# A graph layer with gathered edges: the sums and the turns of a bank of sums ahead of the second layer instead of behind it

## The chip, the core and the metric

The kernel runs on one core of one Trainium2 chip. The metric is the device time of one execution in microseconds (us). Names of the engines: PE is TensorE's matmul side and PEld its weight loads, DVE is VectorE, ACT is ScalarE, POOL is GpSimd, SP is SyncE.

## What is computed

A graph with 6250 nodes of 128 numbers and 100000 edges, sorted by destination (more edges fall on low nodes). Each edge runs a three-layer network on its two nodes; the results are averaged by destination; each node runs a two-layer network on itself and its average; a residual and a layer norm follow.

```python
msg_in = jnp.concatenate([node_features[row], node_features[col]], axis=-1)
h = jax.nn.relu(msg_in @ Wm1 + bm1)              # first layer, 256 -> 256
h = jax.nn.relu(h @ Wm2 + bm2)                   # second layer, 256 -> 256
messages = h @ Wm3 + bm3
agg = jax.ops.segment_sum(messages, col, num_segments=num_nodes)
count = jax.ops.segment_sum(jnp.ones(...), col, num_segments=num_nodes)
agg = agg / jnp.clip(count, 1.0)[:, None]
node_in = jnp.concatenate([node_features, agg], axis=-1)
upd = jax.nn.relu(node_in @ Wn1 + bn1) @ Wn2 + bn2
x = _layernorm(x + node_features + upd)
```

## The kernel before, in words

The product of the first layer is split by node: the product with the source half is made once for every node (a table of 256 numbers a node, `atab`), and so is the one with the destination half (`btab`). An edge needs only the row of its source, and the row of its destination. Since the third layer is linear, the second layer's results are summed by destination before it, and it is applied once a node.

The edges go in 196 groups of 512, one group a step. In step k of the main loop stand, in the order in which the program writes them:

- the **first layer** of group k (`first_layer`): 16 transposes of gathered source rows (L569) into two banks of PSUM, then the **destination products** (L582): rows of `btab` ("terms"), spread to the edges by a matrix of zeros and ones ("oht"). ScalarE applies the relu and makes h1 (L588).
- the gather of the source rows of group k+2 (four indirect DMAs on POOL, L533; four buffers of rows), and, at even steps, the next matrices of zeros and ones on VectorE (L547, L552, `make_hot`).
- the **second layer** of group k-1 (`second_layer`, L596): eight matmuls into two banks, each evicted by VectorE (L598) to a buffer of h2. There are six such buffers, used in turn.
- a stage of the **node work** where one is due (`node_step`: L700, L715, L719, L727 are its matmuls).
- **turns** (`turn_sums`): a finished bank of sums, copied out by ScalarE before (L609), is transposed on TensorE by three matmuls (L617, `turned`). VectorE then adds its windows of 32 nodes into the accumulator `acc` (L624, `add_up`, up to four adds), at places that it loads into registers first (L627).
- **rounds of sums** (`some_sums`, L604): the h2 of up to four windows, each multiplied by its own matrix of zeros and ones that is 32 nodes wide, so that four windows share one bank. There is one such bank in the pool for sums (`p3`). After the last round ScalarE copies the bank out.
- every fourth step, up to step 91, two blocks of the table of destination rows: L904 on TensorE, and their split into three parts on ACT and VectorE (L256 to L260).

How many edge tiles share a window sets the stage. In **quads** (groups 0 to 71, and 184 to 191 at the end) a window takes the four tiles of a group: a bank serves four groups and is summed in four rounds. In **pairs** (72 to 147) a window takes two tiles: a bank serves two groups, two rounds. In **singles** (148 to 183) a bank serves one group in one round. `deal` writes down the step of each round; the turn comes one step after the last round, and a table of due steps for the node stages follows from that.

The order on TensorE, ACT and VectorE is the order of the program. On SP (loads of terms and places, stores) and POOL a scheduler sets it.

Of the kernel before, what the change touches and what calls it, by code (L numbers as in the profile page):

```python
# [36 lines left out]
def kernel(  # L37
# [44 lines left out]
    NG = -(-E // GE)  # L82
# [16 lines left out]
    GL = NG - 2 * LATE  # L99
# [199 lines left out]
    with tc.tile_pool(name="prep", bufs=1) as prep, tc.tile_pool(name="pp", bufs=3, space=PSUM) as pp, tc.tile_pool(  # L299
# [11 lines left out]
        with tc.high_priority():  # L311
# [8 lines left out]
            for n in (4, 8, 8, 8, 8, 8):  # L320
                n = min(n, NTF - t)
# [193 lines left out]
    with edge, tc.tile_pool(name="wk", bufs=2) as wk, tc.tile_pool(  # L515
# [29 lines left out]
        def hot_rows(rb):  # L545
            oht = wk.tile([P, 2, HE], BF16, name="oht")
            nc.vector.tensor_scalar(oht, rb, iota_p, None, op0=ALU.is_equal)  # L547
            return oht
# [91 lines left out]
        def make_hot(p):  # L640
            ohts[p] = hot_rows(rels[p // 2][:, 2 * (p % 2):2 * (p % 2) + 2])
            make_nodes(p)
# [115 lines left out]
        def deal(gs, n, steps):  # L758

            steps = list(steps)  # L760
            for t, k in enumerate(steps):
                rounds.setdefault(k, []).append((gs, t, n))
            at = steps[-1] + 1
            turns_at.setdefault(at, []).append(gs[0])
            added.update({g: at + 1 for g in gs})

        for r0, r1, n in REGIONS:
            m = min(n, GT)
            for g in range(2 * r0, 2 * r1, m):
                if n == GT:  # L770
                    deal(range(g, g + n), n, (g + 4, g + 5, g + 6, g + 6))
                elif n == 1:
                    deal([g], n, (g + 3,))
                elif r1 == PAIRS:
                    deal(range(g, g + n), n, (g + 3, g + 4))
                elif g + n < NG:
                    deal(range(g, g + n), n, (NG - 1, NG - 1))
# [24 lines left out]
        def turn_sums(k):  # L802
            for g in turns_at.pop(k, ()):
                part, nw = parts.pop(g)
                pt = turned(part, nw)
                add_up(pt, load_bases(uniti[0:1, unit_at[g]:unit_at[g] + nw], nw, ENG.DVE))
# [50 lines left out]
        for g in range(-4, NG + 14, 2):  # L857
            for i in range(g + 4, min(g + 6, NG)):
                terms[i] = fetch(load_bases(tilei[0:1, i * GT:(i + 1) * GT], NTS[i], ENG.SP), nk_of(i))
            if g < -2:  # L860
                continue
            if (g + 2) % 4 == 0 and g + 6 < NG:
                rels[(g + 6) // 4] = places((g + 6) // 4)
            if g < 0:
                continue
            if g == 0:
                first_step()
            for k in (g, g + 1):
                if k < NG:
                    s = st[k] = {}  # L870
                    if k == 1:
                        xts[1] = open_layer(None, NTS[1], xts[1])
                    s["h1"] = first_layer(rows.pop(k, None), terms.pop(k), ohts[k // 2][:, k % 2], NTS[k], nk_of(k),
                                          xts.pop(k, None))
                    if k == 0:
                        next_rows()
                    if k == 2:
                        nc.scalar.copy(*pace(5))
                if 2 * XS <= k + 2 < NG:
                    rows[k + 2] = gather(sources(k + 2))  # L880
                if k % 2 == 0 and k + 2 < NG:
                    make_hot(k // 2 + 1)
                if 0 <= k - 1 < NG:
                    second_layer(st.pop(k - 1)["h1"], h2s[(k - 1) % len(h2s)], NTS[k - 1])
                if k < NG:
                    node_step(k)
                if k <= NG:
                    turn_sums(k)
                some_sums(k)
                if k > NG:  # L890
                    turn_sums(k)
                if k % 2 == 0 and 2 <= k and k + 5 < NG:
                    nc.vector.tensor_copy(*pace(k + 5))
                if k >= NG:
                    node_step(k)
            if g < 6:
                clear(8)
            if g == 0:
                more_rows()
            t0 = B_EARLY + (g - B_FROM) // 2  # L900
            if g >= B_FROM and (g - B_FROM) % 4 == 0 and t0 < NT:
                pbt = bank()
                for a in range(min(2, NT - t0)):
                    nc.tensor.matmul(pbt[:, a, :], xT[:, (t0 + a) * P:(t0 + a + 1) * P], w1[:, 1, :],  # L904
                                     start=True, stop=True)
                b_terms(t0, pbt, b_rows, b_rest)
            if g == 18:
                late_weights()
            if g == 60:
                made_weights()  # L910
            if g == NG + 2:
                with tc.high_priority():
                    again = nc.values_load(
                        again_i[0:1, 0:1], min_val=0, max_val=1,
                        skip_runtime_bounds_check_because="0 or 1, by its computation")
# [77 lines left out]
```

## Time and profile before

| | us |
|---|---|
| median of 3 runs | 1343.81 |
| the runs | 1333.75 to 1348.66 |
| the profiled execution's own time | 1338.36 |
| its span, first to last instruction | 1336.6 |
| granted clock of TensorE, mean | 0.981 |

How to read the lines shown below: a group's line has source line, engine, operation, output tile <- input tiles, partitions x elements, how often; behind the bar the busy time in us, the mean duration of one in ns, and the idle time of its engine just before it with what ended it. "issue" is time in which the engine waited for nothing that the profile shows, "remote" a releaser that it doesn't know. In the timeline a line starts with its start and its length in us, and merges like instructions (x16). A matmul in f32 has two records, so the eight of a second layer read x16 and a round of four sums x8. The ends of matmuls are modelled, so lengths overlap; starts are what is compared.

### The profile page before, as it was taken

The numbers are of one execution on the slowest core, as the hardware profiler recorded it, in microseconds if no ns is written. First come the engines' busy times: TensorE is split into PE (matmuls) and PEld (weight loads), VectorE is DVE, ScalarE is ACT, GpSimd is POOL, SyncE is SP. The second block draws the span as 40 slices with busy tenths as digits, with TensorE's granted clock in tenths as the row PEclk, the third lists the DMA queues.
The fourth block names the chain that finished last, engine by engine and source line by source line (L and its number), as shares of the span: only waits on it lengthen the run. The fifth ranks groups of instructions, "written<-read, shape, count | busy, mean of one in ns | idle before, by whom it ended". The sixth has DMA issues, their size and how long they took to land.

```text
span 1336.6 us, 27771 instructions
## 1 busy us (share of the span) xinstructions
PE 1236.1 (92%) x10031; PEld 925.5 (69%) x10032; DVE 618.2 (46%) x1551; ACT 441.9 (33%) x1102; POOL 748.7 (56%) x795
## 2 busy tenths in 40 slices
PE   9779998998999999999899999999999999999997
PEld 7556666666666666676677777777777777777675
DVE  6443333433334333434466554444445556556553
ACT  4432323323323323333333423333233333333331
POOL 2366665665665666656555465565655555555550
PEclk9879999999999999999999999999999999999998
DMA  8544434444434434434444344444444434443330
GB/s 287 177 125 134 132 108 127 130 115 129 133 106 128 135 107 125 134 106 131 126 118 119 114 125 128 118 120 129 118 118 118 115 109 118 109 123 110 106 91 4
DMA packets 107617, 163.90 MB, mean 123 GB/s; under 512 B 26367, under 2 KB 71549, under 8 KB 107457
## 3 DMA queue, kind: packets, MB, share of 16 engines
q0 software_dynamic: 37504, 102.29, 27.7%
q1 hardware_dynamic: 69425, 59.50, 14.0%
q8 instruction: 82, 1.34, 0.4%
q14 instruction: 62, 0.51, 0.1%
q10 hardware_dynamic: 544, 0.26, 0.1%
HBM read 142.48 MB, written 19.86 MB: 121 GB/s over the span
## 4 chain that ended last, share of the span: by engine, by line
PE 89%; issue 7%; DVE 2%; another core or an unknown queue 1%; DMA 1%; ACT 0%; SPq 0%; DVEq 0%
PE bank L596 54%; PE bank L569 9%; PE sum_bank L604 9%; PE bank L582 4%; PE bank L617 2%; PE pbt L431 2%; PE bank L727 2%; PE bank L700 2%; PE bank L719 2%; PE bank L715 2%; PE bank L904 1%; PE pt L448 0%; DVE acc L660 0%; DVE x_sb L598 0%
## 5 line engine op out<-in xcount | busy, mean ns | idle before, releaser
L596 PE MATMUL bank<-w,h 128*128 128x256 f32 x3128 | 768.7, 392 | 67.2 <-issue 64.6
L596 PEld LDWEIGHTS bank<-w,h 128*128 128x128 f32 x3128 | 581.7, 192 | 212.3 <-issue 131.1
L533 POOL DMA_INDIRECT rows<-atab,srcT x392 | 374.9, 956 | 260.6 <-issue 90.4
L533 POOL DMA_INDIRECT rows<-atab,srcP x384 | 364.2, 949 | 277.9 <-issue 126.5
L588 ACT ACTIVATE h<-bank,b 128x256 f32<-128x256 f32 x782 | 306.5, 476 | 395.6 <-remote 189.3
L598 DVE TENSOR_TENSOR x_sb<-bank,nb 128x512 f32<-128x512 f32 x263 | 181.0, 691 | 401.7 <-PE bank L596 233.7
L598 DVE TENSOR_TENSOR h_more<-bank,nb 128x512 f32<-128x512 f32 x128 | 88.3, 692 | 177.5 <-PE bank L596 75.0
L569 PEld LDWEIGHTS bank<-ident,rows 64*128 64x128 f32 x3096 | 112.7, 140 | 77.7 <-issue 56.8
L569 PE MATMUL bank<-ident,rows 64*128 64x64 f32 x3096 | 139.3, 230 | 0.0
L624 DVE TENSOR_TENSOR acc<-acc,bank 128x96 f32 x382 | 96.7, 253 | 51.7 <-PE bank L569 16.5
L604 PE MATMUL sum_bank<-x_sb,oh 128*32 128x257 f32 x1044 | 104.1, 393 | 3.0 <-issue 1.6
L609 ACT COPY part<-sum_bank 128x257 f32<-128x257 f32 x96 | 35.8, 373 | 197.0 <-PE bank L582 75.4
L582 PE MATMUL bank<-oht,terms 64*128 64x128 bf16 (+1 forms) x1132 | 82.6, 237 | 14.5 <-issue 10.9
L604 PE MATMUL sum_bank<-h_more,oh 128*32 128x257 f32 x512 | 59.1, 391 | 1.2 <-DVE h_more L598 0.6
L604 PEld LDWEIGHTS sum_bank<-x_sb,oh 128*32 128x32 f32 x1044 | 28.1, 108 | 41.7 <-issue 34.1
L582 PEld LDWEIGHTS <-terms 64*128 64x128 bf16 x1132 | 44.1, 97 | 16.1 <-issue 13.8
L617 PE MATMUL bank<-ident,part 128*128 128x128 f32 (+1 forms) x291 | 47.3, 271 | 0.5 <-ACT part L609 0.5
L745 ACT ACTIVATE y<-y,sh,rs 128x128 f32<-128x128 f32 (+3 forms) x50 | 22.1, 487 | 67.0 <-DVE sh L743 26.6
L695 DVE RECIPROCAL x_sb<-x_sb 128x256 f32<-128x256 f32 (+3 forms) x26 | 43.0, 1655 | 0.9
L617 PEld LDWEIGHTS bank<-ident,part 128*128 128x128 f32 (+1 forms) x291 | 36.6, 139 | 9.3 <-ACT part L609 1.0
L552 DVE TENSOR_TENSOR oh<-iota_n,dloc 128x256 f32<-128x256 f32 x98 | 40.8, 417 | 3.6 <-ACT dloc L838 3.6
L737 ACT ACTIVATE sd<-mv,eps 128x2 f32<-128x2 f32 (+3 forms) x26 | 7.7, 295 | 97.6 <-DVE mv L735 49.5
(157 smaller groups left out, 625.0 us busy)
## 6 DMA issues: line engine op xcount, KB each, us to landing
terms<-btab SPq DMA_DIRECT2D x566, 32.0 KB
places<-reltab SPq DMA_DIRECT2D x98, 128.0 KB
btab<-x_sb SPq DMA_DIRECT2D x10, 768.0 KB
rows<-atab,srcT POOLq DMA_INDIRECT x392
atab<-acc SPq DMA_DIRECT2D x12, 512.0 KB
rows<-atab,srcP POOLq DMA_INDIRECT x384
xr<-in_x_dram SPq DMA_DIRECT2D x23, 128.0 KB
out_dram<-y SPq DMA_DIRECT2D x23, 128.0 KB
```

The costliest lines, as they stand in the source:

```text
L533: nc.gpsimd.indirect_dma_start(out=ag[:, j, :], out_offset=None, in_=atab[:, :], in_offset=bass.IndirectOffsetOnAxis(ap=idx[:, j:j + 1], a ...
L552: nc.vector.tensor_tensor(oh[:, :ng].rearrange("p g j n -> p (g j) n"), iota.to_broadcast([P, ng * GT, WN]), dl.rearrange("p (j o) -> p j ...
L569: nc.tensor.matmul(ph[h][:, c, u * NQ:(u + 1) * NQ], ag[halves[h], u, c * P:(c + 1) * P], ident[halves[h], halves[h]], is_transpose=True, ...
L582: nc.tensor.matmul(ph[h][:, c, k * n:(k + 1) * n], bw[halves[h], k, c * P:(c + 1) * P], oht[halves[h], k * n:(k + 1) * n], start=False, st ...
L588: nc.scalar.activation(h1[:, c, h * HE:(h + 1) * HE], ph[h][:, c, :], AF.Relu, bias=b1[:, c:c + 1])
L596: nc.tensor.matmul(ph2[:, j - j0, :], h1[:, c, j * P:(j + 1) * P], w2[:, c, :], start=(c == 0), stop=(c == HC - 1))
L598: nc.vector.tensor_tensor(h2[:, j0:j0 + 2, :H], ph2, nb2.to_broadcast([P, 2, H]), op=ALU.max)
L604: nc.tensor.matmul(pg[w * WN:(w + 1) * WN, :H + 1], oh, h2, start=(t == 0), stop=(t == total - 1), skip_group_check=True)
L609: nc.scalar.copy(part[:nw * WN], pg[:nw * WN, :H + 1])
L617: nc.tensor.matmul(pt[:, c, :q], rows, ident[:q, :q], is_transpose=True, start=True, stop=True, skip_group_check=True)
L624: nc.vector.tensor_add(window, window, pt[:, :, j * WN:(j + 1) * WN])
L695: nc.vector.reciprocal(rc, rc)
```

## The change

Two places change. In the loop the turns and rounds of a step now stand between the first layer of group k and the second layer of group k-1; they stood behind that second layer and the node stage. In the last steps (k above 196) the turns keep their place behind the rounds. And in quads, whose rounds came at steps g+4, g+5, g+6 and g+6 (g is the first of four groups), they now come one step later, at g+5, g+6, g+7 and g+7; in the quads at the end (group 184 and up) they come at g+5, g+5, g+6 and g+6. Rounds in pairs and singles keep their step.

```diff
@@ -768,7 +768,7 @@
                 if n == GT:
-                    deal(range(g, g + n), n, (g + 4, g + 5, g + 6, g + 6))
+                    deal(range(g, g + n), n, (g + 5, g + 6, g + 7, g + 7) if g < GL else (g + 5, g + 5, g + 6, g + 6))
                 elif n == 1:
@@ -880,13 +880,13 @@
                 if k % 2 == 0 and k + 2 < NG:
                     make_hot(k // 2 + 1)
+                if k <= NG:
+                    turn_sums(k)
+                some_sums(k)
                 if 0 <= k - 1 < NG:
                     second_layer(st.pop(k - 1)["h1"], h2s[(k - 1) % len(h2s)], NTS[k - 1])
                 if k < NG:
                     node_step(k)
-                if k <= NG:
-                    turn_sums(k)
-                some_sums(k)
                 if k > NG:
                     turn_sums(k)
```

The first place is TensorE in the singles, a step with the first stage of a node piece; h is the second layer's input, w its weights, part a bank of sums that was copied out. Before:

```order
L582 MATMUL bank<-oht,terms 128x128
L596 MATMUL bank<-w_151,h_13457 128x256 x8
L700 MATMUL bank<-acc,w_152 128x256 x2
L617 MATMUL bank<-ident,part 128x128 x3
L604 MATMUL sum_bank<-h_more,oh 32x257 x4
L569 MATMUL bank<-ident,rows 128x64 x16
```

And now:

```order
L582 MATMUL bank<-oht,terms 128x128
L617 MATMUL bank<-ident,part 128x128 x3
L604 MATMUL sum_bank<-h_more,oh 32x257 x4
L596 MATMUL bank<-w_151,h_13457 128x256 x8
L700 MATMUL bank<-acc,w_152 128x256 x2
L569 MATMUL bank<-ident,rows 128x64 x16
```

Turn and sums moved from behind the second layer and the node matmuls to between the destination products and the second layer.

The second place is VectorE in the quads, around the split of two blocks of the destination table (L257, L260) and the turn of a bank (L624); bank holds the second layer's product in L598. Before:

```order
L624 ISA
L624 TENSOR_TENSOR acc<-acc,bank 128x3x32
L257 TENSOR_TENSOR x_sb<-bank,x_sb 128x512
L260 TENSOR_TENSOR x_sb<-x_sb 128x2x256
L547 TENSOR_SCALAR oht<-places,iota_p 128x512
L552 TENSOR_TENSOR oh<-iota_n,dloc 128x256
L598 TENSOR_TENSOR x_sb<-bank,nb_155 128x2x256 x2
L893 COPY srcP<-srcT 128x4
```

And now:

```order
L257 TENSOR_TENSOR x_sb<-bank,x_sb 128x512
L260 TENSOR_TENSOR x_sb<-x_sb 128x2x256
L547 TENSOR_SCALAR oht<-places,iota_p 128x512
L552 TENSOR_TENSOR oh<-iota_n,dloc 128x256
L627 TENSOR_LOAD starts_i
L624 ISA
L624 TENSOR_TENSOR acc<-acc,bank 128x3x32
```

Behind these follow three more such adds, and then the two evictions L598: the adds went from the end of one step to ahead of the evictions of the next.

## Prediction

> **What bounds the kernel now.** I read the page first: busy time by engine, the chain of work that ended last, and the costliest groups.
>
> ```profile
> span 1336.6 us, 27771 instructions
> PE 1236.1 (92%) x10031; PEld 925.5 (69%) x10032; DVE 618.2 (46%) x1551; ACT 441.9 (33%) x1102; POOL 748.7 (56%) x795
> PE 89%; issue 7%; DVE 2%; another core or an unknown queue 1%; DMA 1%; ACT 0%; SPq 0%; DVEq 0%
> L596 PE MATMUL bank<-w,h 128*128 128x256 f32 x3128 | 768.7, 392 | 67.2 <-issue 64.6
> L604 PE MATMUL sum_bank<-x_sb,oh 128*32 128x257 f32 x1044 | 104.1, 393 | 3.0 <-issue 1.6
> L598 DVE TENSOR_TENSOR x_sb<-bank,nb 128x512 f32<-128x512 f32 x263 | 181.0, 691 | 401.7 <-PE bank L596 233.7
> L609 ACT COPY part<-sum_bank 128x257 f32<-128x257 f32 x96 | 35.8, 373 | 197.0 <-PE bank L582 75.4
> ```
>
> TensorE (PE) is the chain: 89% of it, and nearly all the rest is "issue", which falls on the second layer, L596. No other engine is near full. The change takes no instruction off TensorE, so what counts is what the new order does to its gaps.
>
> The next view is busy time by stretch, for the transposes of L569 alone. A step has 16 of them, so the count gives the steps of a stretch. The stretches are quads, pairs without node work, pairs with it, and singles.
>
> ```profile
> 95.50:529.90 434.40, 49.91 (x1120) 40.35 (x1120) 0.99 0.42 124
> 529.90:649.80 119.90, 13.57 (x304) 10.97 (x304) 0.97 0.43 124
> 649.80:1028.10 378.30, 40.61 (x912) 32.81 (x912) 1.00 0.42 120
> 1028.10:1243.60 215.50, 22.79 (x504) 18.41 (x504) 1.00 0.41 114
> ```
>
> A step takes 434.4/70 = 6.21 us in the quads, then 6.31, 6.64 and 6.84. The granted clock is 0.97 to 1.00, so the clock explains none of it.
>
> How much of a step is matmul work shows in the timeline of the quads. Here are TensorE's weight loads, and the start of each group of four gathers on GpSimd.
>
> ```profile
> 380.11 0.46 PEld L617 LDWEIGHTS bank<-ident,part 128*128 128x128 f32 x3
> 386.12 0.16 PEld L604 LDWEIGHTS sum_bank<-x_sb,oh 128*32 128x32 f32 x8 [0.33 <-issue]
> 386.69 0.57 PEld L569 LDWEIGHTS bank<-ident,rows 64*128 64x128 f32 x16 [0.41 <-issue]
> 387.55 3.32 PEld L596 LDWEIGHTS bank<-w,h 128*128 128x128 f32 x16 [0.21 <-issue]
> ...
> 390.28 0.94 POOL L533 DMA_INDIRECT rows<-atab,srcP  x1 [1.29 <-PE bank L596]
> 391.77 0.58 PEld L569 LDWEIGHTS bank<-ident,rows 64*128 64x128 f32 x16 [0.41 <-issue]
> 396.35 0.94 POOL L533 DMA_INDIRECT rows<-atab,srcT  x1 [1.38 <-remote]
> ```
>
> From 386.69 to 391.77 a step takes 5.08 us. Two groups of gathers start 6.07 us apart meanwhile (390.28 and 396.35). So a short quad step is quicker than something that keeps a beat of about 6.1 us, and TensorE runs ahead and gives it back as "issue" gaps. What sets the beat the trace does not say. That matters below: work saved or added on TensorE in a stage with such gaps need not show in full.
>
> **The change part by part.** First, shapes. A group of matmuls runs in one of three array shapes: 64\*128 (L569, L582: first layer), 128\*128 (L596, turns L617, node work, L904) and 128\*32 (sums, L604). In the rows above each load that opens a new shape waits 0.21 to 0.41 us, and L617, which follows L596 in the same shape, shows no wait. The price is read from starts on TensorE, in three places:
>
> ```profile
> 501.57 0.49 PE L617 MATMUL bank<-ident,part 128*128 128x128 f32 x3
> 501.89 1.03 PE L904 MATMUL bank<-w,xT 128*128 128x256 f32 x4
> 502.86 0.72 PE L569 MATMUL bank<-ident,rows 64*128 64x64 f32 x16
> ...
> 528.85 1.13 PE L904 MATMUL bank<-w,xT 128*128 128x256 f32 x4
> 529.92 0.71 PE L569 MATMUL bank<-ident,rows 64*128 64x64 f32 x16
> ...
> 891.27 0.71 PE L569 MATMUL bank<-ident,rows 64*128 64x64 f32 x16
> 892.13 3.72 PE L596 MATMUL bank<-w,h 128*128 128x256 f32 x16
> 895.69 0.49 PE L617 MATMUL bank<-ident,part 128*128 128x128 f32 x3
> 896.11 0.64 PE L604 MATMUL sum_bank<-x_sb,oh 128*32 128x257 f32 x8
> 896.68 0.71 PE L569 MATMUL bank<-ident,rows 64*128 64x64 f32 x16
> ```
>
> Three L617 take 0.32 us to the next group of their shape (501.57 to 501.89) and 0.42 to a group of another (895.69 to 896.11): leaving costs 0.10. Four L904 take 0.97 us behind L617 (501.89 to 502.86) and 1.07 where sums stand ahead of them (528.85 to 529.92): entering costs 0.10. A change of shape costs 0.20.
>
> A step with sums and no turn has three changes in both orders: 128\*128, 128\*32, 64\*128 before; 128\*32, 128\*128, 64\*128 now. Nothing is gained or lost, if the one neighbourhood that the trace does not show (L582 straight into L604) is like the others; at 0.1 us more or less for each of the 95 such steps it is -9.5 to +9.5 us, and I take 0, since each of the changes that are shown costs about the same. A step with turn and sums had its turn next to the second layer, in one shape; now turn (128\*128), sums (128\*32) and second layer (128\*128) alternate, four changes for three. Such a step, 5.41 us long (891.27 to 896.68), becomes 5.61. Counted over the program's order, the changes go from 574 to 641. The 67 more lie in the pairs and singles, where turns and sums share a step; in the quads the turn has a step of its own. 67 x 0.20 = +13.4 us on TensorE, with bounds of 0 (all of it inside gaps) and 67 x 0.25 = 16.8.
>
> The Trainium skill, TensorEngine Tiling (Array Packing), section Tiling Modes, says that changing the tiling mode, not merely the tile, drains TensorE. The trace agrees, at the 0.20 us above.
>
> How much of that is hidden? These are TensorE's waits in the stretch of pairs with node work (first two) and in the singles (last two):
>
> ```profile
> PE bank L596 <- issue: 11.4, 20, 1.2
> PE bank L582 <- issue: 5.4, 9, 1.2
> ...
> PE bank L596 <- issue: 6.5, 12, 0.9
> PE bank L582 <- issue: 3.7, 5, 1.2
> ```
>
> That is 16.8 us over 57 steps and 10.2 over 31.5, 0.3 a step, more than the 0.20 or, with pairs, the 0.10 a step that is added. But many steps there carry node matmuls and show no gap, and nothing hides work in those. I take half: 6.7 us paid.
>
> Second, the sums' own wait. The first round of a quad needs the eviction (L598) of the second layer that TensorE has just finished. In a bad step:
>
> ```profile
> 503.72 3.72 PE L596 MATMUL bank<-w,h 128*128 128x256 f32 x16
> 507.37 0.41 PE L604 MATMUL sum_bank<-x_sb,oh 128*32 128x257 f32 x2
> 507.45 0.69 DVE L598 TENSOR_TENSOR h_more<-bank,nb 128x512 f32<-128x512 f32 x1 [0.56 <-PE bank L596]
> 508.19 0.62 PE L604 MATMUL sum_bank<-h_more,oh 128*32 128x257 f32 x2 [0.19 <-issue]
> 508.74 0.58 PEld L569 LDWEIGHTS bank<-ident,rows 64*128 64x128 f32 x16 [0.41 <-PE bank L596]
> ```
>
> The eviction ends at 508.14, and the last sums follow at 508.19. From 507.37 to 508.74 is 1.37 us for a group that takes 0.57 (896.11 to 896.68): 0.80 lost. The waits of this stage are these:
>
> ```profile
> PE sum_bank L604 <- issue: 2.2, 9, 0.5
> PE sum_bank L604 <- DVE h_more L598: 0.6, 2, 0.4
> ```
>
> Eleven times 0.80 is 8.8 us; with one in each of the 18 quads it would be 14.4. Now the first round comes a step later, behind the first layer (386.69 to 387.55: 0.86 us), which covers 0.80. But the turn moves too: its four adds into acc (L624) now stand in VectorE's queue ahead of those two evictions, in the very step whose eviction the round needs.
>
> ```profile
> 381.13 1.12 DVE L624 TENSOR_TENSOR acc<-acc,bank 128x96 f32 x4
> ```
>
> Where the adds have not begun by the time the second layer's first bank is full, 1.12 us comes on top, and the cover is gone. Also this is the stage with the 6.1 us beat. I take half the gain, -4.4, bounds 0 and -14.4. VectorE's register load for the adds (L627) moves with them; it has no busy row, and in the row above the adds follow the eviction at once, so I give it nothing.
>
> Third, small things. At the end, the sums of the last group had a turn and other sums (1 us) between them and the last second layer; now nothing, so they wait for an eviction of 0.69 us and its start: +0.9. Where quads give way to pairs, the last round of a quad and the first of a pair fall in one step and share the one sum buffer, so a copy of 0.37 (L609) stands between: +0.4. The copy, one step ahead of its turn as before, has a whole second layer (3.56 us, 892.13 to 895.69) as cover. On SyncE half of some loads of places and the stores of out come one load of terms or one group later; they are fetched steps ahead, and I give that 0. No node stage begins in another step: their due steps lie behind the sums' end either way.
>
> Sum: 6.7 - 4.4 + 0.9 + 0.4 = +3.6 us on 1338.4 us, the profiled execution's own time (span 1336.6 and 1.8 around it). That execution lies 5.4 us under the median of the runs, 1343.8. So I forecast 1343.8 + 3.6 = 1347 us.
>
> **The rivals.**
>
> *Every shape change is paid (slower).* Place: the 67 steps of pairs and singles with turn and sums. If the gaps of those stages stay beside the new work instead of taking it in, all 13.4 to 16.8 us is added, and if the eviction behind the adds keeps the sums waiting, nothing comes back. With 1.3 for the small things: 1343.8 + 16 = 1360 us. It decides from the point where the shape changes paid, less the waits won, exceed 12.1 us (1% of the run is 13.4, and 1.3 come from the small things). For it: steps with node work have no gap. Against it: 0.3 us of gap a step. Chance 0.28. The rule of the Trainium skill on tiling modes (TensorEngine Tiling (Array Packing), Tiling Modes) would give this outcome, if nothing hid the drains.
>
> *The sums fill the gap (faster).* The sums need nothing fresh and stand where TensorE goes over to the second layer; in the quads L596 carries most of the "issue" time. If the sums' wait goes whole (-9 to -14) and the later second layer meets fewer gaps, with half of the shape changes hidden, the sum is -8 to -20; at -16 it is 1328 us. Against it: gathers at 6.1 us, whose beat an order on TensorE does not obviously touch. Chance 0.24.
>
> *The beat rules (no change).* The quads keep 6.21 us whatever TensorE does there, and half the shape changes show: +8, 1352 us. The forecast and this one together: 0.48.
>
> **How the numbers follow.** Within 1% of 1343.8, about what a measurement of this kernel can tell from no change, means 1330 to 1357. The forecast and the beat lie there: 0.48. Faster by more than 1% is the second rival, 0.24, and slower the first, 0.28. The likeliest case by itself spans 1338 to 1355. For 8 in 10 the range has to reach into both rivals: 1327 to 1361 us, which holds the paid shape changes up to 16.8 and the filled gap down to -16.
>
> **What would show it.** Right: in the singles a turn-and-sum step of about 5.6 us where it was 5.41, with L617 to L604 still at 0.42 and 0.10 more ahead of L569; fewer waits of L604 in the quads; fewer "issue" gaps in pairs and singles; quads still near 6.2 us a step. Wrong: quads well below 6.1 us a step (the beat was TensorE's own), L604 or L617 waiting for VectorE's or ScalarE's work in many steps, or late stages that grow by the full 0.2 us a step.

## The result: slower by 3.85%

The changed kernel takes 1393.3 us (median of four, 1391.9 to 1394.1) where the kernel before, on the same chip, takes 1341.9 (four, 1333.8 to 1348.7). The ratio is 1.0385, with a 95% interval of 1.0324 to 1.0445: 51 us more, where 3.6 had been forecast. The page of the changed kernel, in the lines that answer to those of before:

```profile
span 1390.9 us, 27706 instructions
PE 1283.9 (92%) x10031; PEld 944.0 (68%) x10032; DVE 609.8 (44%) x1551; ACT 431.8 (31%) x1102; POOL 750.7 (54%) x795
PE 89%; issue 7%; DVE 2%; another core or an unknown queue 1%; DMA 1%; ACT 0%; SPq 0%; DVEq 0%; ACTq 0%
L596 PE MATMUL bank<-w,h 128*128 128x256 f32 x3128 | 761.3, 395 | 24.3 <-issue 23.0
L604 PE MATMUL sum_bank<-x_sb,oh 128*32 128x257 f32 x1044 | 130.4, 404 | 20.2 <-issue 16.4
L598 DVE TENSOR_TENSOR x_sb<-bank,nb 128x512 f32<-128x512 f32 x263 | 179.8, 691 | 426.9 <-PE bank L596 204.6
```

The shares of the chain are the same as before, 89% TensorE and 7% "issue". But the gaps have moved. The second layer (L596) waited 67.2 us and now waits 24.3, while the sums (L604) waited 3.0 and now wait 20.2. In all TensorE is idle for 107.0 us (1390.9 - 1283.9) where it was idle for 100.5. So most of the loss stands as busy time, 1283.9 us for 1236.1, with the same 10031 matmuls: their ends are modelled, and a late start shows as a gap only where it is later than the modelled end before it. TensorE's waits in the changed kernel (us in all, times, longest) name the others:

```profile
PE bank L596 <- issue: 23.0, 40, 1.8
PE sum_bank L604 <- issue: 19.9, 48, 1.1
PE bank L617 <- issue: 13.6, 20, 2.2
PE bank L582 <- issue: 12.3, 25, 1.2
PE bank L569 <- issue: 11.5, 17, 1.2
```

Before, L617 waited 0.5 us and L569 nothing that the list shows. Whatever stands right behind the first layer now meets the gap. By stage (the transposes of L569 alone, the same steps as in the prediction: quads, pairs without node work, pairs with it, singles):

```profile
91.56:536.31 444.75, 51.72 (x1120) 41.02 (x1120) 0.96 0.42 123
536.31:656.33 120.02, 13.77 (x304) 10.96 (x304) 0.99 0.41 119
656.33:1053.45 397.12, 40.65 (x912) 32.85 (x912) 1.00 0.40 115
1053.45:1291.78 238.33, 23.83 (x504) 18.73 (x504) 0.96 0.36 103
```

Against the rows of before the quads take 444.8 us for 434.4 (+10.4), the plain pairs 120.0 for 119.9, the pairs with node work 397.1 for 378.3 (+18.8) and the singles 238.3 for 215.5 (+22.8). With -3.9 ahead of them and +6.1 behind them that is the 54.3 us between the two spans. In quads and singles the granted clock is 0.96, where it was 0.99 and 1.00.

The price of the shapes shows in a turn-and-sum step without a gap, in TensorE's timeline of the changed kernel:

```profile
541.92 0.71 PE L569 MATMUL bank<-ident,rows 64*128 64x64 f32 x16
542.48 0.38 PE L582 MATMUL bank<-oht,terms 64*128 64x256 bf16 x4
542.79 0.55 PE L617 MATMUL bank<-ident,part 128*128 128x128 f32 x3
543.26 0.64 PE L604 MATMUL sum_bank<-x_sb,oh 128*32 128x257 f32 x8
543.84 3.72 PE L596 MATMUL bank<-w,h 128*128 128x256 f32 x16
547.49 0.72 PE L569 MATMUL bank<-ident,rows 64*128 64x64 f32 x16
```

It lasts 5.57 us where it lasted 5.41: 0.16 us for one more change of shape, and 67 x 0.16 = 10.7 us for them all. That is a fifth of the loss.

### The profile page after: what moved, and what is told of

Same layout as the page of the kernel before. It is cut to its first block, busy times and chain, and to the rows that moved or that the text cites. A ratio compares the mean times of both kernels' runs of the same rounds, so it can differ in the third digit from the quotient of the medians.

```text
span 1390.9 us, 27706 instructions
## 1 busy us (share of the span) xinstructions
PE 1283.9 (92%) x10031; PEld 944.0 (68%) x10032; DVE 609.8 (44%) x1551; ACT 431.8 (31%) x1102; POOL 750.7 (54%) x795
## 4 chain that ended last, share of the span: by engine, by line
PE 89%; issue 7%; DVE 2%; another core or an unknown queue 1%; DMA 1%; ACT 0%; SPq 0%; DVEq 0%; ACTq 0%
PE bank L596 52%; PE sum_bank L604 10%; PE bank L569 9%; PE bank L617 4%; PE bank L582 4%; PE bank L727 2%; PE pbt L431 2%; PE bank L719 2%; PE bank L700 2%; PE bank L715 2%; PE bank L904 1%; DVE x_sb L598 1%; DVE h_more L598 0%; PE pt L448 0%
## 5 line engine op out<-in xcount | busy, mean ns | idle before, releaser
L596 PE MATMUL bank<-w,h 128*128 128x256 f32 x3128 | 761.3, 395 | 24.3 <-issue 23.0
L596 PEld LDWEIGHTS bank<-w,h 128*128 128x128 f32 x3128 | 594.9, 196 | 191.5 <-issue 103.7
L598 DVE TENSOR_TENSOR x_sb<-bank,nb 128x512 f32<-128x512 f32 x263 | 179.8, 691 | 426.9 <-PE bank L596 204.6
L598 DVE TENSOR_TENSOR h_more<-bank,nb 128x512 f32<-128x512 f32 x128 | 87.6, 691 | 207.1 <-PE bank L596 113.2
L569 PEld LDWEIGHTS bank<-ident,rows 64*128 64x128 f32 x3096 | 113.4, 139 | 72.4 <-issue 62.9
L569 PE MATMUL bank<-ident,rows 64*128 64x64 f32 x3096 | 142.2, 229 | 11.6 <-issue 11.5
L604 PE MATMUL sum_bank<-x_sb,oh 128*32 128x257 f32 x1044 | 130.4, 404 | 20.2 <-issue 16.4
L624 DVE TENSOR_TENSOR acc<-acc,bank 128x96 f32 x382 | 96.9, 254 | 71.2 <-PE bank L596 20.9
L582 PE MATMUL bank<-oht,terms 64*128 64x128 bf16 (+1 forms) x1132 | 83.4, 239 | 13.9 <-issue 12.3
L604 PEld LDWEIGHTS sum_bank<-x_sb,oh 128*32 128x32 f32 x1044 | 34.0, 110 | 67.7 <-issue 47.7
L604 PE MATMUL sum_bank<-h_more,oh 128*32 128x257 f32 x512 | 68.8, 400 | 5.8 <-issue 3.5
L617 PE MATMUL bank<-ident,part 128*128 128x128 f32 (+1 forms) x291 | 56.2, 295 | 14.0 <-issue 13.6
L582 PEld LDWEIGHTS <-terms 64*128 64x128 bf16 x1132 | 43.2, 97 | 22.3 <-issue 20.4
L617 PEld LDWEIGHTS bank<-ident,part 128*128 128x128 f32 (+1 forms) x291 | 30.9, 141 | 30.9 <-issue 24.6
L745 ACT ACTIVATE y<-y,sh,rs 128x128 f32<-128x128 f32 (+3 forms) x50 | 22.1, 486 | 87.1 <-DVE sh L743 75.4
L737 ACT ACTIVATE sd<-mv,eps 128x2 f32<-128x2 f32 (+3 forms) x26 | 7.7, 296 | 131.0 <-DVE mv L735 89.8
L609 ACT COPY part<-sum_bank 128x257 f32<-128x257 f32 x96 | 37.3, 389 | 24.3 <-remote 12.9
```

The source lines that it names most:

```text
L569: nc.tensor.matmul(ph[h][:, c, u * NQ:(u + 1) * NQ], ag[halves[h], u, c * P:(c + 1) * P], ident[halves[h], halves[h]], is_transpose=True, ...
L582: nc.tensor.matmul(ph[h][:, c, k * n:(k + 1) * n], bw[halves[h], k, c * P:(c + 1) * P], oht[halves[h], k * n:(k + 1) * n], start=False, st ...
L596: nc.tensor.matmul(ph2[:, j - j0, :], h1[:, c, j * P:(j + 1) * P], w2[:, c, :], start=(c == 0), stop=(c == HC - 1))
L598: nc.vector.tensor_tensor(h2[:, j0:j0 + 2, :H], ph2, nb2.to_broadcast([P, 2, H]), op=ALU.max)
L604: nc.tensor.matmul(pg[w * WN:(w + 1) * WN, :H + 1], oh, h2, start=(t == 0), stop=(t == total - 1), skip_group_check=True)
L609: nc.scalar.copy(part[:nw * WN], pg[:nw * WN, :H + 1])
```

## The experiments

Three theories. "Cover" in them is the other work that TensorE does while something that it will need is being made. **Shapes:** the 67 more changes of array shape cost 0.16 us each, and nothing hides them. **S:** the sums now read rows that the second layer of the step before has just left, and wait for their eviction (L598). **N:** ScalarE's two operations of a node stage that wait for VectorE (L737, L745) have lost cover, and hold back the relus that stand behind them.

The runs fell on chips of two kinds, and nothing below can be read without that. The first eight, and the two kernels of the result, ran where the kernel before takes about 1320 to 1345 us; the last ten where it takes 1189.5 to 1189.9. Every ratio is against the kernel before on the same chip. "Kind of chip" is no more than a name here: each set of runs had a chip of its own, and the slower sets came first, so the record doesn't show whether it is the chip or something that changed in the meantime.

The diffs are shortened: `...` stands for code that is left out, and the guards `if k <= NG`, `if k < NG` and `if 0 <= k - 1 < NG` are not printed everywhere.

### One part at a time: e1 to e4

**e1**: rounds later, but turns and sums behind the second layer as before.

```diff
-                    deal(range(g, g + n), n, (g + 4, g + 5, g + 6, g + 6))
+                    deal(range(g, g + n), n, (g + 5, g + 6, g + 7, g + 7) if g < GL else (g + 5, g + 5, g + 6, g + 6))
```

> The quads' rounds and turn one step later, as in the change, but turns and sums behind the second layer and the node work, as before. Shapes alone (0.155 us for each more change of array shape): 587 changes for 574, +2 us, so about 1344. Order theory (the loss of 51 us comes from what now stands ahead of the second layer): no loss here, 1335 to 1350. Rival, the later rounds themselves (a turn and its adds meet another step's work): 1360 or more.

**e2** and **e3**: the change up to the last turn of the quads only, and from there on only. In e3 the rounds of the first quads are those of before, in e2 those of the few quads at the end.

```diff
+                ahead = k <= 76          # e3: k >= 76
+                if ahead: turn_sums(k); some_sums(k)
                 second_layer(...); node_step(k)
+                if not ahead: turn_sums(k); some_sums(k)
```

> The changed kernel up to the last turn of the quads, the order of before from the pairs on. By the stages of the changed kernel's profile (start -4.1, quads +6.9): about 1345, if what the late stages lost is their own. Rival: the quads leave the engines in a worse phase and the late stages lose although their order is the old one: 1370 or more. Shapes alone (572 changes for 574): 1342.

> The order and rounds of before up to the last turn of the quads, the changed order from there on. If the loss belongs to the pairs and singles (+51 us by the stages of the profile: plain pairs +6.5, pairs with node work +15.7, singles +20.4, end +8.8): 1385 to 1395. Shapes alone (643 changes for 574, 69 x 0.155 = +10.7): 1352. Rival, a phase that the quads hand on: 1355 to 1365, half of the loss.

**e4**: the changed kernel, with the turns alone moved back.

```diff
-                if k <= NG:
-                    turn_sums(k)
                 some_sums(k)
                 second_layer(...); node_step(k)
+                if k <= NG:
+                    turn_sums(k)
```

> The changed kernel with the turns (transposes and adds) back behind the second layer and the node work; only the sums and their copy stay ahead of it. Theory A, the turns' adds ahead of the evictions in VectorE's queue cause the loss: it goes, 1335 to 1348. Theory B, the sums ahead of the second layer cause it (they need evicted rows a step earlier on TensorE's clock, and no longer cover the evictions): 1380 to 1393 stays. Shapes alone (566 changes for 574): 1341.

Measured, on one chip (before 1322.0): e1 1335.0 us, ratio 1.011 (1.0078 to 1.0142); e2 1330.8, 1.0042 (1.0014 to 1.0069); e3 1370.9, 1.0348 (1.0304 to 1.0391); e4 1383.4, 1.0437 (1.0388 to 1.0486).

The loss belongs to the pairs and singles, as e3 expected, and hardly to the quads. The two halves, 0.4% and 3.5%, add up to the 3.85% of the whole, which was timed on another chip. e4 goes against theory A of its expectation: VectorE's adds ahead of the evictions are not the cause, since with the turns back, and with eight changes of shape fewer than before, the loss is whole. Sums ahead of the second layer are enough.

e1 is more than 1% slower for a reason of its own. There are six buffers of h2, and with the sums behind the second layer the last two rounds of a quad read the buffer of its first group just after the second layer of six groups later has overwritten it. So these rounds sum other rows than the reference does (the work is the same), and they wait for an eviction right ahead of them. TensorE's waits in the quads of e1:

```profile
PE sum_bank L604 <- DVE h_more L598: 10.5, 5, 2.7
PE sum_bank L604 <- DVE x_sb L598: 9.2, 7, 2.7
```

So e1 does not measure later rounds alone. The same holds for e5, below, where these two waits are 18.7 us.

### The mirror, and the node work: e5, e6, e7, e9

**e5**: the changed kernel with the sums alone moved back.

```diff
                 turn_sums(k)
-                some_sums(k)
                 second_layer(...); node_step(k)
+                some_sums(k)
```

> The mirror of the run with only the sums ahead: turns ahead of the second layer, sums and their copy behind it and the node work, rounds as in the change. With the turns harmless, as that run says: beside the run with later rounds alone, 1335 +- 8 us. If turns and sums each cost by what they put ahead: 1355 to 1375. Shapes alone (587 changes for 574): 1.002 of before.

**e6**: the changed kernel with the node work ahead of the second layer.

```diff
                 turn_sums(k); some_sums(k)
+                node_step(k)
                 second_layer(...)
-                node_step(k)
```

> The changed kernel with the node work between the sums and the second layer, no longer behind it; the changes of shape stay 641. Theory N, the node stage's operations on ScalarE (L737, L745) wait for VectorE's part of that stage, which now has only the next first layer as cover, and hold the relus of the next step behind them: the cover is a whole second layer here, so the late stages lose only their shapes (about 10 us) and the quads stay: 1.005 to 1.015 of before. Rival, the sums themselves ahead of the second layer (banks, evicted rows needed sooner): 1.03 to 1.045 stays.

**e7** and **e9**: the kernel before with the node work last, and with it first.

```diff
+                node_step(k)        # e9
                 second_layer(...)
-                node_step(k)
                 turn_sums(k); some_sums(k)
+                node_step(k)        # e7
```

> The kernel before with its node work last in a step, behind turn and sums; rounds as before. The sums stay behind the second layer. Theory N: the node work loses turn and sums as cover just as in the change, so 1.02 to 1.04 of before, in the pairs with node work and the singles, with longer waits of L737 and L745. Rival, the sums ahead of the second layer: nothing but shapes (638 changes for 574, 64 x 0.155 = 10 us): 1.00 to 1.01.

> The kernel before with its node work ahead of the second layer; 574 changes of shape, as before. Theory N: the waits of L737 and L745 (49.5 and 26.6 us in all before) go, and the stages with node work gain: 0.98 to 0.995 of before. Rival, the sums: no change, 0.995 to 1.005.

Measured, on another chip (before 1322.5): e5 1364.1, 1.0304 (1.0264 to 1.0343); e6 1364.4, 1.0325 (1.0289 to 1.0362); e7 1337.0, 1.0101 (1.0069 to 1.0134); e9 1315.6, 0.9937 (0.9914 to 0.996).

e5 falsified "the turns are harmless". Its waits on TensorE name a cause that the change itself does not have:

```profile
PE bank L617 <- ACT part L609: 58.7, 55, 3.1
```

With the sums last in a step and the turn right behind the next first layer, the copy of the bank (L609) has only that first layer as cover, and TensorE waits 55 times for it.

e6 kept most of the loss, so theory N alone is not the cause. But its stages say more than its sum. These are the singles of e3 (there the order of the change, node work last) and then of e6 (the same with node work ahead of the second layer):

```profile
1033.80:1272.00 238.20, 24.14 (x504) 19.21 (x504) 0.96 0.35 103
```

```profile
1037.89:1261.78 223.89, 22.84 (x504) 18.46 (x504) 0.99 0.38 110
```

With the turns and sums behind the second layer the singles take 209.8 us (e1) and 211.3 (e2) on the chip of e3, and 209.5 on that of e6 (e9, with the node work ahead), and the kernel before takes 1322.0 and 1322.5 there, so the two chips can be compared. Moving the node work ahead takes 14 of some 28 us off, and the clock is back at 0.99. Each figure is from one profiled execution, and the runs of e6 spread over 9 us, so the 14 us are rough. What is left is 32 x 0.16 = 5.1 us of shapes and a new wait, that of the node stage's first matmuls for the adds of the turn right ahead of them, in e6:

```profile
PE bank L700 <- DVE acc L624: 15.4, 17, 1.7
```

Of that wait 7.4 us lie in the singles. In the pairs with node work e6 won little: 388.7 us, for 391.4 in e3, 392.2 in e4, and 375.4 in e9. e7 loses 14.5 us, of which its 64 changes of shape are 10.2: node work behind the turn and the sums does little harm by itself while the sums stay behind the second layer. e9 is faster than the kernel before, by 0.6%.

### Signals that come late, and signals that come at once

Why should one microsecond of sums on the other side of the second layer matter at all? What ends an engine's wait in these rows is a signal (a semaphore) from another engine. This is a step in the quads of the kernel before:

```profile
387.24 0.38 PE L582 MATMUL bank<-oht,terms 64*128 64x256 bf16 x4
387.55 3.72 PE L596 MATMUL bank<-w,h 128*128 128x256 f32 x16
390.15 1.57 ACT L588 ACTIVATE h<-bank,b 128x256 f32<-128x256 f32 x4 [4.55 <-PE bank L596]
390.22 0.69 DVE L598 TENSOR_TENSOR h_more<-bank,nb 128x512 f32<-128x512 f32 x1 [3.22 <-PE bank L596]
391.31 0.69 DVE L598 TENSOR_TENSOR h_more<-bank,nb 128x512 f32<-128x512 f32 x1 [0.40 <-PE bank L596]
```

The relu needs L582 and nothing else that is late; ScalarE has been idle for 4.55 us. TensorE goes over to L596 at 387.55, yet the relu starts at 390.15, 2.60 us later. It starts together with the eviction of the second layer's first half. And the second half follows 1.09 us behind the first, where the same two evictions stand 1.72 us apart below. So against TensorE's rows the signals for the relu and for the first half come late, and together; that for the second half, 3.76 us behind the start of L596, doesn't. Whether a signal is held back, or TensorE's work runs behind its rows, the trace doesn't tell. Over the quads, the median from the next group's start on TensorE to a relu of an idle ScalarE is 3.7 us in the kernel before (56 relus) and 2.6 in the changed one (51).

Now the changed kernel on a chip of the other kind (f1, below):

```profile
458.87 0.38 PE L582 MATMUL bank<-oht,terms 64*128 64x256 bf16 x4
459.18 0.64 PE L604 MATMUL sum_bank<-x_sb,oh 128*32 128x257 f32 x8
459.35 1.57 ACT L588 ACTIVATE h<-bank,b 128x256 f32<-128x256 f32 x4 [3.99 <-PE bank L582]
459.75 3.72 PE L596 MATMUL bank<-w,h 128*128 128x256 f32 x16
461.79 0.69 DVE L598 TENSOR_TENSOR h_more<-bank,nb 128x512 f32<-128x512 f32 x1 [2.08 <-PE bank L596]
463.40 0.71 PE L569 MATMUL bank<-ident,rows 64*128 64x64 f32 x16
463.51 0.69 DVE L598 TENSOR_TENSOR h_more<-bank,nb 128x512 f32<-128x512 f32 x1 [1.03 <-PE bank L596]
```

The relu starts 0.17 us behind L582's successor, the evictions 2.04 and 3.76 us behind the start of L596, and so it goes in nearly every step: the median lag of the relus in its quads is again 0.16 to 0.17 us (51). The step takes 463.40 - 458.32 (the transposes' start just above) = 5.08 us, the next begins at once, and no beat of 6.1 us is left: a quad step takes 5.36 us on average (375.5/70).

The Trainium skill, Perfetto Trace Analysis, section Summary: the profiler window per engine type, says that for TensorE the window runs from the start of its prefetch to an estimated end, and that the spreading of the semaphore is hidden. The rows agree that the end of a TensorE row does not date the signal: in f1 the relu starts 0.10 us behind the end of L582's row (459.25 to 459.35), in the kernel before 2.53 us (387.62 to 390.15).

The slower kind has a second mark, in TensorE's own starts. These are sums in the quads of the changed kernel:

```profile
269.16 0.62 PE L604 MATMUL sum_bank<-h_more,oh 128*32 128x257 f32 x3
269.38 0.69 DVE L598 TENSOR_TENSOR x_sb<-bank,nb 128x512 f32<-128x512 f32 x1 [4.67 <-PE bank L582]
270.09 0.38 PE L604 MATMUL sum_bank<-h_more,oh 128*32 128x257 f32 x1 [0.31 <-issue]
271.00 0.39 PE L604 MATMUL sum_bank<-x_sb,oh 128*32 128x257 f32 x1 [0.54 <-issue]
271.71 0.38 PE L604 MATMUL sum_bank<-x_sb,oh 128*32 128x257 f32 x1 [0.32 <-issue]
272.43 0.40 PE L604 MATMUL sum_bank<-x_sb,oh 128*32 128x257 f32 x1 [0.34 <-issue]
273.15 0.38 PE L604 MATMUL sum_bank<-x_sb,oh 128*32 128x257 f32 x1 [0.32 <-issue]
273.49 1.57 ACT L588 ACTIVATE h<-bank,b 128x256 f32<-128x256 f32 x4 [5.04 <-remote]
```

The eviction ends at 270.07 and the next matmul starts right behind it. But nothing ends on VectorE or ScalarE in the three microseconds after that, and still four matmuls start 0.7 us apart, where eight take 0.58 us in the step without a gap (543.26 to 543.84). Over the four stages a matmul of the sums is followed 0.4 us later or more 12 times in the kernel before, 99 times in the changed one and once in f1. Of the 99, which take 67 us, 30 (18 us) end with an eviction that ended at most 0.12 us earlier; for 59 (43 us) nothing on VectorE or ScalarE had just ended. So most of this holding is not the wait of theory S. What holds TensorE there no trace shows.

The time from the start of each group on TensorE to the start of the next, summed over the four stages (us; changes of shape are in it), says where the loss stands:

| group | before | changed | changed, f1 |
|---|---|---|---|
| sums, L604 | 111.5 | 173.5 | 101.4 |
| second layer, L596 | 715.4 | 681.4 | 640.6 |
| destination products, L582 | 88.8 | 77.9 | 56.0 |
| transposes, L569 | 98.5 | 111.4 | 97.9 |
| turns, L617 | 35.5 | 51.2 | 40.4 |
| node work and table | 98.5 | 105.0 | 102.0 |

The sums alone take 62 us more than before, and the second layer gives 34 back.

### The remedies, and the change where signals come at once

**e8** and **f3** (the same kernel): the changed kernel without ScalarE's root and scaling in a node stage.

```diff
-            nc.scalar.activation(sd[:r, :n], mv[:r, :n, 1], AF.Sqrt, bias=eps[:r])
+            sd = mv[:, :, 1]
...
-            for i in range(n):
-                nc.scalar.activation(y[:r, i, :], ...)
```

**e11**, **f2** and **g1**: the changed kernel with rounds later still. **e12**: e11 with the node work ahead of the second layer. **e10**, **f4** and **g2**: e11's rounds in the order sums, node work, second layer, turns. **f1**: the changed kernel itself.

```diff
-  (g + 5, g + 6, g + 7, g + 7) if g < GL else ...     # quads
+  (g + 6, g + 6, g + 7, g + 7) if g < GL else ...
-  deal(range(g, g + n), n, (g + 3, g + 4))            # pairs
+  deal(range(g, g + n), n, (g + 4, g + 5))
```

> The changed kernel without the two operations of a node stage on ScalarE that wait for VectorE's part of that stage: the root (L737) and the scaling of the output rows (L745) are left out, so the output rows go out unscaled; all else stays. Theory N (these two wait for VectorE behind the evictions of a second layer that now ends the step, and hold the next relus back): the singles lose 12 to 17 us of their +20, the pairs with node work a few, and the whole falls to 1.015 to 1.025 of before. Rival (the relus are late for another reason): 1.03 to 1.04 stays.

> The changed kernel with rounds yet later: quads at g+6, g+6, g+7, g+7, pairs at g+4, g+5, so that no sum reads rows that the second layer of the step before has left; eight node stages begin one step later; 622 changes of shape. Theory S (sums ahead of the second layer wait for the evictions of the step before, which had a whole second layer more as cover): L604's waits go in quads and pairs, some 25 us in these two stages; with the singles left as they are (+20): 1.015 to 1.025 of before. Rival (the gaps at L604 are TensorE's own, wherever the sums stand): 1.035 or more, the gaps at L604 stay.

> Both remedies: node work ahead of the second layer and the later rounds of the run before. Theories S and N together: what stays is the changes of shape (622 for 574, 48 x 0.155 = 7.4 us) and the new wait of L700 for the adds L624 ahead of it (some 10 us): 1.005 to 1.015. If the loss has a third part, as large: 1.02 or more.

> Sums, node work, second layer, turns, in this order, with the later rounds: both remedies, and the turn beside the second layer in one shape, so that only 548 changes of shape are left (26 fewer than before, -4 us), and no adds right ahead of L700. Theories S and N: no slower than the kernel before, 0.985 to 1.003, and it may stand beside the run with nodes first (0.994). Rival, anything ahead of the second layer costs: 1.02 or more.

> The changed kernel once more, beside the next three on one chip. Where TensorE's signals come late (an idle ScalarE starts a relu some 2 to 4 us behind the last record of L582, kernel before at 1320 to 1345 us): 1.035 to 1.045 of before. Where they come at once (0.16 us, kernel before at 1190 us): theories S and N have little to wait for, and the shapes stay, 67 x 0.155 = 10 us: 1.007 to 1.012.

> Rounds later still, so that no sum reads rows of the step before. Late signals: theory S, 1.015 to 1.025 of before, 15 to 25 us under the changed kernel, all of it in quads and pairs; rival, 1.035 to 1.045. Signals at once: 1.0086 as measured.

> The changed kernel without the root (L737) and the scaling of the output rows (L745) on ScalarE, which wait for VectorE. Late signals: theory N, the singles lose 12 to 17 us and the whole is 1.020 to 1.030 of before; rival, 1.035 to 1.045. Signals at once: 1.0088 as measured.

> Sums, node work, second layer, turns, with rounds later still: both remedies and 548 changes of shape for 574. Late signals: theories S and N, 0.985 to 1.005 of before; if anything ahead of the second layer costs there, 1.02 or more. Signals at once: 1.002 as measured.

> As before on chips whose signals come late (kernel before at 1320 us or more): theory S, 1.015 to 1.025 of before; rival, 1.035 to 1.045, as the changed kernel. With signals at once: 1.008 again.

> Late signals: theories S and N together, 0.985 to 1.005 of before; if anything ahead of the second layer costs there, 1.02 or more. With signals at once: 1.002 again.

All of them fell on chips where signals come at once. Before takes 1189.9, 1189.9 and 1189.5 us in the three sets.

| kernel | us | ratio to before (95%) | changes of shape |
|---|---|---|---|
| before | 1189.9 | 1 | 574 |
| changed (f1) | 1202.8 | 1.0102 (1.0085 to 1.0119) | 641 |
| without L737, L745 (e8) | 1200.9 | 1.0088 (1.0071 to 1.0105) | 641 |
| the same (f3) | 1200.7 | 1.0084 (1.0067 to 1.0101) | 641 |
| rounds later still (e11) | 1200.5 | 1.0086 (1.0069 to 1.0103) | 622 |
| the same (f2) | 1200.4 | 1.0082 (1.0065 to 1.0098) | 622 |
| the same (g1) | 1200.1 | 1.0087 (1.0070 to 1.0104) | 622 |
| rounds later still, nodes ahead (e12) | 1212.1 | 1.0184 (1.0167 to 1.0201) | 621 |
| sums, nodes, second layer, turns (e10) | 1192.1 | 1.0021 (1.0011 to 1.0030) | 547 |
| the same (f4) | 1192.0 | 1.0017 (1.0007 to 1.0027) | 547 |
| the same (g2) | 1192.3 | 1.0024 (1.0014 to 1.0033) | 547 |

The changed kernel loses 12.9 us here, not 51, and its profile has no gaps to show for it. Its chain, and the longest of TensorE's waits:

```profile
PE 96%; SPq 1%; DMA 1%; DVE 1%; issue 0%; ACT 0%; DVEq 0%
```

```profile
PE bank L569 <- DMA rows<-atab,srcT: 1.8, 2, 1.4
PE bank L700 <- DVE acc L624: 1.2, 1, 1.2
```

Sixty-seven changes at 0.16 us are 10.7 of the 12.9 us. Taking 19 of them away (f2 beside f1) takes 2.4 us off, for 3.0 worked out, though the two intervals overlap. So here the shapes are most of the loss, in full. They are not all that counts: with 27 changes fewer than before (the expectation has 26), f4 should gain 4 us and loses 2.1, and only 3.0 us of that is a wait that shows (L700 for the adds). e12 has the same wait, and there it is large:

```profile
PE bank L700 <- DVE acc L624: 11.1, 16, 1.2
```

Theories S and N find little to do here. Leaving out L737 and L745 moved the ratio from 1.0102 to 1.0084, within the intervals. Yet ScalarE waits for VectorE in f1 longer, in the sum of these two lines, than in the result's run. First the result's kernel, then f1:

```profile
ACT sd L737 <- DVE mv L735: 89.8, 17, 6.5
ACT y L745 <- DVE sh L743: 75.4, 21, 5.4
```

```profile
ACT sd L737 <- DVE mv L735: 126.6, 25, 5.5
ACT y L745 <- DVE sh L743: 72.9, 26, 3.5
```

A long wait of ScalarE is no loss by itself. It may become one where the signal that ends it, and the next one that releases the relu, come microseconds late; no run here shows that by itself.

**What stays open.** No remedy but e6 was timed where signals come late. So S is not tested there by a run, only by the starts above, which leave most of the held sums without an eviction to wait for; and N is tested by e6 alone. The expectations of e8, e10, e11 and e12 were written for such chips; that they came out low there proves neither theory. Where signals come late, the changed kernel loses 51 us, of which 10.7 are shapes, and the other 40 belong to the sums' and turns' new place (e3, e4), but how much of the 40 is S, how much N, and how much is TensorE held by something that no trace shows, is not settled. The last is the rival that the expectation of e11 names ("the gaps at L604 are TensorE's own"), and the starts speak for it. Why one order meets more of it than the other, and what makes the signals late, stays open too.

## Why the prediction was wrong, point by point

Three steps failed. The largest: for the pairs and singles the sum has no term but the shapes, so the new place of turns and sums was put at nothing there; these stages lost 41.7 us in the result's run, of which 10.7 are shapes, and e3 and e4 show that the place of the sums is what costs. The second is "I take half: 6.7 us paid". The third is the -4.4 for the sums' own wait.

- **The half.** The shapes were sized at 13.4 us (0.20 each) and measured 10.7 (0.16 each); that part of the mechanism held. The Trainium skill, TensorEngine Tiling (Array Packing), section Tiling Modes, says that a change of tiling mode drains TensorE; the 0.16 us a change of shape agree. "I take half: 6.7 us paid" failed: it took the "issue" gaps for room that fills up when work comes. Where signals come at once, 12.9 us of loss show and no gap is there to hide any. Where they come late, the gaps did not take the new work in; they moved behind the first layer, with it, and TensorE was idle for 107.0 us in place of 100.5.
- **The neighbourhood not seen**, L582 straight into L604: 0 was right. In f1 a step with sums and no turn takes 5.08 us, as before.
- **The sums' own wait, -4.4.** Wrong in sign: the quads took 10.4 us more. In them the sums took 74.1 us from their start to the next group's, for 49.8, and L604's "issue" waits went from 9 to 48 in the whole kernel; e2, the quads alone, lost 0.4%. Evictions that end later than the 0.86 us of cover are a part of it, but the smaller one (30 of the 99 late starts). The adds ahead of the evictions, which the prediction feared, were not the cause (e4).
- **Pairs.** The prediction looked at S in the quads alone. In the pairs, too, the first round reads rows of the step before, and there the change gave no step more, so the sums lost a whole second layer as cover. The sums there take 77.8 us from their start to the next group's, for 43.5 before: that is the term that was missing. That the lost cover is the reason is not shown, since most held sums do not follow an eviction.
- **The node work** is named nowhere in the prediction's sum but for its due steps. Sums and turn had stood between a second layer and the next first layer, as cover for the way from eviction over L741 and L743 to L745 and the relus (theory N). e6 shows what moving the node work is worth in the singles, some 14 us; e7, node work last with the sums left in place, lost only 4 us beyond its shapes.
- **The copy L609.** "A whole second layer as cover" held: TensorE's waits for it are 0.5 us before and not among the listed ones after. Without that cover it costs 58.7 us (e5).
- **Small things.** The end was to cost 0.9 us; from the last single on it took 6.1 more. Which part of it is the last sums was not tried.
- **The beat.** As an observation right, as a bound half right. Quads take 6.1 to 6.4 us a step in all ten kernels where signals come late, whatever the order; where they come at once, 5.4 or less (375.5/70 in f1). So the beat was no property of the program, and it did not protect the late stages. What sets it is not shown.
- **The rivals.** "Every shape change is paid" had the sign, and its 16 us is near the 12.9 of f1. For the chip of the result it is too small by a factor of three. The signs named for a wrong forecast came in part: L604 and L617 wait in many steps, though mostly for nothing that the profile shows ("issue") and not for VectorE or ScalarE, and the late stages grow by more than 0.2 us a step, 0.3 in the pairs with node work (18.8/57) and 0.7 in the singles (22.8/32).

## What to carry to other kernels

Before moving work on a full engine, list what it covers where it stands: here the new place of sums of one microsecond cost nearly four times the changes of shape. Do not take gaps for room: here they moved with the work. Compare starts on TensorE and not only its gaps, because modelled ends hide late starts. And measure how late an idle engine starts behind the last row of TensorE that it needs, because that lag, not the rows' ends, says how much cover a dependence must have. Last, time a rival order on more than one chip: the same two kernels stood 3.85% apart on one and 1.0% on another.

## What the runs showed of the hardware that was not expected

The same kernel takes 1322 to 1342 us on some chips and 1190 on others, at a granted clock of 0.98 to 0.99 and of nearly 1.00, so the clock explains some 1 to 2 of the 11 to 13 per cent. The records of a quad step without gaps are the same on both, 5.08 us. What differs is how long behind those records ScalarE and VectorE are released, 0.17 us or up to several us, and how often TensorE's starts are held: over the four stages a matmul starts 0.4 us or more behind the one before it 200 times in the kernel before and 287 times in the changed one on the slower kind, and once in f1.

On chips where signals come late, the granted clock is lower in the changed kernel as well: 0.965 in the profiled execution for 0.981 before, and (1 - 0.965) x 1390.9 - (1 - 0.981) x 1336.6 = 23 us of full speed are missing. Whether the stalls bring the clock down or the clock the stalls is not shown. But the four runs of the changed kernel have 0.965 to 0.975 at 1392 to 1394 us, so their time does not follow the clock, and e3 loses 3.5% at 0.977.

A change of array shape costs 0.16 us in a chain of matmuls with no gaps, where it was put at 0.20 from single neighbourhoods.

Node work ahead of the second layer, in the order of before (e9), gave 0.6% on a chip with late signals: the fastest order there. It was not timed on the other kind.
